# Attention and two quantized convolutions: values times exponentials by Strassen's seven products in column halves of TensorE

## The chip, the cores and the metric

The kernel runs on one core of one Trainium2 chip. The metric is the device time of one execution in microseconds (us), as the median of several runs.

Engines are called by their names in the profile: PE is TensorE's matmul, PEld its weight load, DVE VectorE, ACT ScalarE.

## The reference

The input is x, 16 images of 128 channels and 32 x 32 places (1024 columns when flat), all in fp32. The first layer is attention with 4 heads of 128 channels; the second is two quantized convolutions with batch norms over the whole batch.

```python
# layer 0, for each image and head: n, m are the 1024 places
q, k, v = split(einsum('bchw,oc->bohw', x, w_qkv) + b_qkv)
scores  = einsum('bnc,bcm->bnm', q, k) * c ** (-0.5)
attn    = softmax(scores, axis=-1)
out     = einsum('bnm,bmc->bnc', attn, v)
x       = einsum('bchw,oc->bohw', out_of_all_heads, w_out) + b_out + x
# layer 1
out = conv3x3(act_quant(x), weight_quant(w1))       # 4 bits, so exact in bf16
out = batchnorm(out, gamma1, beta1)                 # statistics over all 16 images
out = conv3x3(act_quant(out), weight_quant(w2))
x   = batchnorm(out, gamma2, beta2) + x
```

## The kernel before

It is already tuned. The weights of queries and keys are folded into one matrix (`at_sb`), those of values and output projection into another (`bt_sb`). Each of the 64 heads then needs: u from x (2 products of 128 x 128 weights by 512 columns), scores of 8 key blocks (16 products), exponentials on ScalarE, and values times exponentials (16 products); the values of all heads of an image cost 8 more. All of these are fp32. VectorE adds the exponentials up for the softmax's denominator and normalises. The first convolution of an image runs in between, in bf16; the second, after all images, takes the last 95 us. A list of steps places every small part of the work between scores and attends. These are the parts that the change touches, with cuts:

```python
xp, vp   = pool("x", 3), pool("vo", NCH + 3)        # NCH = 8 key blocks
ep, esp  = pool("e", 4), pool("es", 2)
ps_s = pool("ps_s", 2, space=PSUM)                  # tiles of N columns, two banks each
ps_a = pool("ps_a", 1, space=PSUM)                  # two accumulators of HALF
ps_m = pool("ps_m", 2, space=PSUM)

def project_v(b, j):
    ps = ps_m.tile([P, NH * P], F32, tag="mm", name=f"psv_{b}_{j}")
    nc.tensor.matmul(ps, lhsT=xt[b][:, ts(j, P)], rhs=bt_sb..., start=True, stop=True)
    vos[b, j] = vp.tile([P, NH * P], F32, tag="vo", name=f"vo_{b}_{j}")
    nc.vector.tensor_copy(vos[b, j], ps)

def scores(g, j):
    ps = ps_s.tile([P, N], F32, tag="s", name=f"pss_{g}_{j}")
    for m, (key, queries) in enumerate(parts):       # two halves of the queries
        last = nc.tensor.matmul(ps[:, ts(m, HALF)], lhsT=xt[b][:, ts(key, P)],
                                rhs=us[g][:, queries], start=True, stop=True)
    e = ep.tile([P, N], F32, tag="e", name=f"e_{g}_{j}")
    exps[:] = [nc.scalar.activation(e, ps, AF.Exp).ins]
    # ...

def attend(g, j):
    for m in range(NHF):
        nc.tensor.matmul(psa[g][m], lhsT=vos[b, j][:, ts(h, P)], rhs=e[:, ts(m, HALF)],
                         start=(j == 0), stop=(j == NCH - 1))
    # ... VectorE: es[g] += e

def six_products(p, s, i):        # first convolution, two images p at a time, F(4,3) by columns
    m = four_products(...)        # 4 bf16 products of 256 columns
    # ... seven or more VectorE operations that put the outputs together
```

Of the kernel before, what the change touches and what calls it, by code (L numbers as in the profile page):

```python
# [17 lines left out]
FIRST = 24.0  # L18
# [9 lines left out]

SUM_LIMIT = 1e20

# [160 lines left out]
def fast_path(  # L191
    nc, tc, x, wqk, wvo, bo, bnp, x1d, out, bo_sb, bnp_sb, quad, wq, sc, flag, conv_weights,
    constants,
):

# [38 lines left out]
    y2 = [keep.tile([P, 2, N], F32, name=f"y{b}") for b in range(0, B, 2)]  # L234
    ys = [y2[b // 2][:, b % 2] for b in range(B)]
# [109 lines left out]
    def check_sums():  # L345

        sums_range(B - 1)
        ok = keep.tile([P, 2], F32, name="ok")
        low, high = keep.tile([P, 1], F32, name="low"), keep.tile([P, 1], F32, name="high")
        nc.vector.tensor_reduce(low, ext[:, 0, :], AX.X, ALU.min)  # L350
        nc.vector.tensor_reduce(high, ext[:, 1, :], AX.X, ALU.max)
        nc.vector.tensor_scalar(ok[:, 0:1], low, 1.0 / SUM_LIMIT, None, ALU.is_ge)
        nc.vector.tensor_scalar(ok[:, 1:2], high, SUM_LIMIT, None, ALU.is_le)
        bad = keep.tile([P, 1], F32, name="bad")
        nc.vector.tensor_tensor(bad, ok[:, 0:1], ok[:, 1:2], ALU.mult)
        nc.vector.tensor_scalar(bad, bad, -1.0, 1.0, ALU.mult, ALU.add)
        worst = keep.tile([P, 1], F32, name="worst")
        nc.gpsimd.partition_all_reduce(worst, bad, P, bass_isa.ReduceOp.max)
        nc.vector.tensor_copy(flag, worst[0:1, :])

    with ExitStack() as ph:
        pool = lambda name, bufs, **kw: ph.enter_context(tc.tile_pool(name=name, bufs=bufs, **kw))
        once = pool("once", 1)
        xp = pool("x", 3)
        up = pool("u", 2)
        vp = pool("vo", NCH + 3)
        ep = pool("e", 4)
        esp = pool("es", 2)
        avp = pool("av", 2)
        smp = pool("small", 4)  # L370
        rbp = pool("rb", 1)
        rest = pool("rest", 1)
        accp = pool("acc", 1)
        ps_s = pool("ps_s", 2, space=PSUM)
        ps_a = pool("ps_a", 1, space=PSUM)
        ps_m = pool("ps_m", 2, space=PSUM)

        xt, us, vos, es, avs, psa, accs = {}, {}, {}, {}, {}, {}, {}
        exps, sums_added, scored, attended, quantized = [], [], [], [], []
        heads = [(b, h) for b in range(B) for h in range(NH)]  # L380

# [24 lines left out]
        def warm_up(n):  # L406
# [3 lines left out]
            for _ in range(n):  # L410
                nc.tensor.matmul(ps, lhsT=ones[:, 0:P], rhs=ones, start=True, stop=True)
# [4 lines left out]
        bt_sb = once.tile([P, NH, P], F32, name="bt_sb")  # L416

        def fold_a(h):
            wq_h, wk_h, bq_h = wqk_sb[:, h, 0:P], wqk_sb[:, h, P : 2 * P], wqk_sb[:, h, 2 * P :]
            ps = ps_m.tile([P, P + 1], F32, tag="mm", name=f"ps_a_{h}")  # L420
            bias = ps[:, P:]
            if h == 0:

                bias = ps_a.tile([P, 1], F32, tag="a1", name="ps_a_bias")
            nc.tensor.matmul(ps[:, 0:P], lhsT=wq_h, rhs=wk_h, start=True, stop=True)
            nc.tensor.matmul(bias, lhsT=wk_h, rhs=bq_h, start=True, stop=True)
# [3 lines left out]
        def fold_b():  # L430
            ps = ps_m.tile([P, NH, P], F32, tag="mm", name="ps_b")
            for h in range(NH):
                nc.tensor.matmul(
                    ps[:, h, :],
                    lhsT=wvo_sb[:, h, 0:P],
                    rhs=wvo_sb[:, h, P : 2 * P],
                    start=True,
                    stop=True,
                )
            nc.scalar.copy(bt_sb, ps)  # L440

        def fold_bo():
            ps = ps_m.tile([P, 1], F32, tag="mm", name="ps_bo")
            for h in range(NH):
                nc.tensor.matmul(
                    ps,
                    lhsT=wvo_sb[:, h, P : 2 * P],
                    rhs=wvo_sb[:, h, 2 * P :],
# [5 lines left out]
        bo2_sb = once.tile([P, 1], F32, name="bo2_sb")  # L454

        def project_u(g, hf):
            b, h = heads[g]
            if hf == 0:
                us[g] = up.tile([P, N], F32, tag="u", name=f"u_{g}")
            ps = ps_m.tile([P, HALF], F32, tag="mm", name=f"psu_{g}_{hf}")  # L460
            nc.tensor.matmul(  # L461
                ps, lhsT=at_sb[:, h, :], rhs=xt[b][:, ts(hf, HALF)], start=True, stop=True
            )
            dst = us[g][:, ts(hf, HALF)]
            if hf == 0:
# [6 lines left out]
        def project_v(b, j):  # L472
            ps = ps_m.tile([P, NH * P], F32, tag="mm", name=f"psv_{b}_{j}")
            nc.tensor.matmul(  # L474
                ps,
                lhsT=xt[b][:, ts(j, P)],
                rhs=bt_sb.rearrange("p h o -> p (h o)"),
                start=True,
                stop=True,
            )  # L480
            vos[b, j] = vp.tile([P, NH * P], F32, tag="vo", name=f"vo_{b}_{j}")
            nc.vector.tensor_copy(vos[b, j], ps)  # L482

        def scores(g, j):

            b, h = heads[g]
            ps = ps_s.tile([P, N], F32, tag="s", name=f"pss_{g}_{j}")
            if g == LAST:
                i, keys = group_step(j)
                lo, hi = GROUPS[i]  # L490
                parts = [(key, slice(lo, hi)) for key in keys]
            else:
                parts = [(j, ts(m, HALF)) for m in range(NHF)]
            for m, (key, queries) in enumerate(parts):
                last = nc.tensor.matmul(  # L495
                    ps[:, ts(m, N // len(parts))],
                    lhsT=xt[b][:, ts(key, P)],
                    rhs=us[g][:, queries],
                    start=True,
                    stop=True,  # L500
                )
            scored[:] = [last.ins]
            e = ep.tile([P, N], F32, tag="e", name=f"e_{g}_{j}")
            if (g, j) == (LAST, NCH - 1):
                for m in range(NHF):
                    nc.scalar.activation(e[:, ts(m, HALF)], ps[:, ts(m, HALF)], AF.Exp)
            else:
                exps[:] = [nc.scalar.activation(e, ps, AF.Exp).ins]  # L508
            es[g, j] = e

        def attend(g, j):
            b, h = heads[g]
            e = es[g, j]
            if j == 0:
                psa[g] = [
                    ps_a.tile([P, HALF], F32, tag=f"a{m}", name=f"psa_{g}_{m}") for m in range(NHF)
                ]
            for m in range(NHF):
                nc.tensor.matmul(  # L519
                    psa[g][m],  # L520
                    lhsT=vos[b, j][:, ts(h, P)],
                    rhs=e[:, ts(m, HALF)],
                    start=(j == 0),
                    stop=(j == NCH - 1),
                )
            if j == 1:
                es[g] = esp.tile([P, N], F32, tag="es", name=f"es_{g}")
                nc.vector.tensor_tensor(es[g], es.pop((g, 0)), es.pop((g, 1)), ALU.add)  # L528
            elif j > 1:
                added = nc.vector.tensor_tensor(es[g], es[g], es.pop((g, j)), ALU.add)  # L530
                sums_added[:] = [added.ins]
            if j == NCH - 1:
                avs[g] = avp.tile([P, N], F32, tag="av", name=f"av_{g}")
                nc.vector.tensor_copy(avs[g][:, ts(0, HALF)], psa[g][0])
                nc.scalar.copy(avs[g][:, ts(1, HALF)], psa[g][1])  # L535
                es[g, "part"] = quadrant_sums(es.pop(g))
# [13 lines left out]

        def inverse_sums(g, part, cut):
# [3 lines left out]
            if g == LAST:  # L555
# [3 lines left out]
                for i in range(w):  # L559
                    product = nc.tensor.matmul(  # L560
                        ps, lhsT=quad, rhs=part[:, ts(i, n)], start=(i == 0), stop=(i == w - 1)
                    )
                attended[:] = [product.ins]
                nc.vector.reciprocal(rinv, ps)
            else:
# [5 lines left out]
                nc.vector.tensor_reduce(total, side.rearrange("p a k -> p k a"), AX.X, ALU.add)  # L571
                nc.vector.reciprocal(rinv[0:Q, :], total)
# [8 lines left out]
        def normalise(g):  # L581
            b, h = heads[g]
            rb = inverse_sums(g, es.pop((g, "part")), slice(0, N))
# [6 lines left out]
            nc.vector.tensor_tensor(accs[b], accs[b], av, ALU.add)  # L590
            if h == NH - 1:
                nc.vector.scalar_tensor_tensor(xt[b], accs.pop(b), bo2_sb, xt[b], ALU.add, ALU.add)
                nc.sync.dma_start(out=x1d[b], in_=xt[b])
            elif g == LAST - 1:
                nc.vector.scalar_tensor_tensor(x1, accs.pop(b), bo2_sb, xt[b], ALU.add, ALU.add)
# [3 lines left out]
        LAST = len(heads) - 1  # L599
        GROUPS = [(0, HALF), (HALF, 3 * N // 4), (3 * N // 4, N)]  # L600
        FIRST_STEP = [0, NCH // 2, 3 * NCH // 4, NCH]
        x1 = rest.tile([P, N], F32, name="x1")
        sides, rbs = [], {}

        def group_step(j):

            i = max(k for k in range(len(GROUPS)) if FIRST_STEP[k] <= j)
            wide = N // (GROUPS[i][1] - GROUPS[i][0])
            return i, [wide * (j - FIRST_STEP[i]) + m for m in range(wide)]

        def attend_group(j):
            b, h = heads[LAST]
            e = es.pop((LAST, j))
            i, keys = group_step(j)
            n = GROUPS[i][1] - GROUPS[i][0]
            if j == FIRST_STEP[i]:
                ps = ps_a.tile([P, HALF], F32, tag=f"a{i % NHF}", name=f"psa_{LAST}_{i}")
                psa[LAST, i] = ps[:, 0:n]
                if i % NHF == 0:
# [724 lines left out]
```

## Time and profile before

| | before |
|---|---|
| time, median of 2 runs | 2105.22 us (2104.58 to 2105.87) |
| TensorE busy | 98% of the span |
| VectorE busy | 1508 us, 72% |
| ScalarE busy | 726 us, 35% |
| interval from one image's residual to the next | 124.85 us |
| second convolution, first product to the end | 94.6 us |

The busy table, the slices and the main groups of instructions are in the prediction below and are read there. Four more groups matter for the change. In the view of groups by shape, a line gives: source line, engine, operation, output<-input, shapes, number of instructions | busy us, mean ns of one | idle us of the engine just before them, and what ended it.

```profile
L482 DVE COPY vo<-psv 128x512 f32<-128x512 f32 x128 | 88.1, 689 | 194.7 <-PE psv L474 194.7
...
L753 DVE TENSOR_TENSOR tiles<-work 128x256 bf16<-128x256 bf16 x168 | 38.8, 288 | 0.0
L785 DVE TENSOR_TENSOR six<-wino 128x512 f32<-128x512 f32 x42 | 28.8, 686 | 0.0
L762 PE MATMUL psw<-tiles,wino 128*128 128x256 bf16 x184 | 27.6, 273 | 0.0
```

The first is the copy of the values to SBUF, on VectorE. The next two are the largest pieces of the first convolution's transforms on VectorE; all of its pieces together, over the seven pairs of images, are some 265 us, 18.9 us an image. The last is that convolution's products: only 27.6 us of TensorE. So the old first convolution was very cheap on TensorE and dear on VectorE.

### The profile page before, as it was taken

To read this page: it belongs to the slowest core of one execution; us is meant where nothing else is said; L and a number is where in the kernel's file an instruction comes from. 1 tells how busy PE (TensorE), PEld (TensorE's weight loads), DVE (VectorE), ACT (ScalarE), POOL (GpSimd) and SP (SyncE) were. 2 spreads that over 40 slices of the span, in tenths; PEclk is the share of its full clock that TensorE was granted. 3 is DMA by queue.
4 is the path that set the end of the run, shared out by engine and by line. 5 is a ranking of instruction groups with operands and counts; after the bars stand their busy time and mean duration, and the time that the engine had idled before them with its cause. 6 is when DMAs were issued, how large, how long until landed. Compare 5 with 4: busy or idle time off the path is not lost. (4 is left out here: it accounts for less than half of the span.)

```text
span 2103.3 us, 14858 instructions
## 1 busy us (share of the span) xinstructions
PE 2070.2 (98%) x5184; PEld 933.2 (44%) x5185; DVE 1508.2 (72%) x2434; ACT 726.4 (35%) x832; POOL 21.3 (1%) x29
## 2 busy tenths in 40 slices
PE   9999999999999999999999999999999999999994
PEld 4444444444444444444444444444444444444451
DVE  4775577766687676876769657776668767687888
ACT  2333233333333323333333323333333332333375
POOL 0000000000000000000000000000000000000020
PEclk9999999999999999999999999999999999999997
DMA  2000000000000000000000000000000000000044
GB/s 62 12 20 0 0 20 1 20 0 10 10 0 20 0 20 0 0 21 0 20 0 21 0 0 20 1 20 0 8 12 0 20 1 10 0 0 10 0 170 162
DMA packets 11155, 36.83 MB, mean 18 GB/s; under 512 B 1344, under 2 KB 1728, under 8 KB 11072
## 3 DMA queue, kind: packets, MB, share of 16 engines
q1 hardware_dynamic: 7872, 25.76, 3.2%
q10 hardware_dynamic: 3200, 10.03, 1.6%
q8 instruction: 43, 0.70, 0.1%
q14 instruction: 40, 0.33, 0.1%
HBM read 19.01 MB, written 16.78 MB: 17 GB/s over the span
## 5 line engine op out<-in xcount | busy, mean ns | idle before, releaser
L508 ACT ACTIVATE e<-pss 128x1024 f32<-128x1024 f32 x511 | 522.8, 1023 | 1287.6 <-PE pss L495 1267.6
L495 PE MATMUL pss<-u,x 128*128 128x512 f32 (+1 forms) x2064 | 962.4, 589 | 0.0
L519 PE MATMUL psa<-e,vo 128*128 128x512 f32 x2016 | 947.8, 592 | 0.0
L530 DVE TENSOR_TENSOR es<-es,e 128x1024 f32<-128x1024 f32 x378 | 461.6, 1221 | 293.8 <-ACT e L508 292.5
L495 PEld LDWEIGHTS pss<-u,x 128*128 128x128 f32 x2064 | 392.1, 190 | 487.2 <-issue 471.2
L519 PEld LDWEIGHTS psa<-e,vo 128*128 128x128 f32 x2016 | 379.1, 190 | 458.7 <-issue 454.2
L482 DVE COPY vo<-psv 128x512 f32<-128x512 f32 x128 | 88.1, 689 | 194.7 <-PE psv L474 194.7
L461 PE MATMUL psu<-x,at_sb 128*128 128x512 f32 x256 | 131.1, 594 | 0.8 <-DMA x<-in_x_dram 0.7
L474 PE MATMUL psv<-bt_sb,x 128*128 128x512 f32 x256 | 130.2, 592 | 0.0
L466 DVE TENSOR_SCALAR u<-psu,au_sb 128x512 f32<-128x512 f32 x64 | 48.0, 750 | 51.2 <-PE psu L461 51.2
L542 DVE TRANSPOSE_TENSOR_REDUCE part<-es 128x32 f32<-128x1024 f32 (+1 forms) x66 | 80.6, 1221 | 2.2
L528 DVE TENSOR_TENSOR es<-e,e 128x1024 f32<-128x1024 f32 x63 | 76.9, 1220 | 6.4 <-ACT e L508 6.4
L578 DVE STREAM_TRANSPOSE rb<-sums 128x1024 f32<-128x1024 f32 (+1 forms) x66 | 79.9, 1211 | 1.5
L461 PEld LDWEIGHTS psu<-x,at_sb 128*128 128x128 f32 x256 | 48.6, 191 | 62.0 <-issue 58.6
L474 PEld LDWEIGHTS psv<-bt_sb,x 128*128 128x128 f32 x256 | 48.6, 190 | 61.2 <-issue 55.7
L589 DVE TENSOR_TENSOR av<-av,rb 128x1024 f32<-128x1024 f32 x47 | 57.5, 1223 | 1.9
L590 DVE TENSOR_TENSOR acc<-acc,av 128x1024 f32<-128x1024 f32 x47 | 57.3, 1219 | 0.5
L769 ACT ACTIVATE wino<-psw 128x512 f32<-128x512 f32 x92 | 49.8, 599 | 0.0
L535 ACT COPY av<-psa 128x512 f32<-128x512 f32 x63 | 36.9, 585 | 33.3 <-PE psa L519 33.3
L569 DVE COPY side<-part 32x32 f32<-32x32 f32 x252 | 42.9, 170 | 4.7
L276 PE MATMUL psc<-pad,wq 128*128 128x512 bf16 (+3 forms) x225 | 45.0, 357 | 0.3 <-DVE pad L1002 0.3
L468 ACT ACTIVATE u<-psu,au_sb 128x512 f32<-128x512 f32 x64 | 43.6, 682 | 2.4 <-PE psu L461 2.4
(172 smaller groups left out, 857.8 us busy)
## 6 DMA issues: line engine op xcount, KB each, us to landing
x_dram<-x SPq DMA_DIRECT2D x16, 512.0 KB, 2.6
x<-in_x_dram ACTq DMA_DIRECT2D x15, 512.0 KB, 3.7
res<-x_dram SPq DMA_DIRECT2D x1, 7680.0 KB, 23.7
out_dram<-y SPq DMA_DIRECT2D x11, 512.0 KB, 4.4
out_dram<-y SPq DMA_DIRECT2D x9, 256.0 KB, 2.3
raw<-in_cw_dram ACTq DMA_DIRECT2D x2, 576.0 KB, 3.7
res<-x_dram SPq DMA_DIRECT2D x1, 512.0 KB, 3.4
wqk_sb<-in_wqk_dram ACTq DMA_DIRECT2D x1, 385.5 KB, 3.1
```

The costliest lines, as they stand in the source:

```text
L461: nc.tensor.matmul(ps, lhsT=at_sb[:, h, :], rhs=xt[b][:, ts(hf, HALF)], start=True, stop=True)
L474: nc.tensor.matmul(ps, lhsT=xt[b][:, ts(j, P)], rhs=bt_sb.rearrange("p h o -> p (h o)"), start=True, stop=True,)
L482: nc.vector.tensor_copy(vos[b, j], ps)
L495: last = nc.tensor.matmul(ps[:, ts(m, N // len(parts))], lhsT=xt[b][:, ts(key, P)], rhs=us[g][:, queries], start=True, stop=True,)
L508: exps[:] = [nc.scalar.activation(e, ps, AF.Exp).ins]
L519: nc.tensor.matmul(psa[g][m], lhsT=vos[b, j][:, ts(h, P)], rhs=e[:, ts(m, HALF)], start=(j == 0), stop=(j == NCH - 1),)
L528: nc.vector.tensor_tensor(es[g], es.pop((g, 0)), es.pop((g, 1)), ALU.add)
L530: added = nc.vector.tensor_tensor(es[g], es[g], es.pop((g, j)), ALU.add)
L542: nc.vector.tensor_reduce(part, total.rearrange("p (k c) -> p k c", c=Q), AX.X, ALU.add, apply_transpose=True,)
L578: nc.vector.transpose(rb, rinv.unsqueeze(2).to_broadcast([P, n, Q]))
L589: nc.vector.tensor_tensor(av, av, rb, ALU.mult)
L590: nc.vector.tensor_tensor(accs[b], accs[b], av, ALU.add)
```

## The change

The intent is to take products off TensorE. Values times exponentials for two key blocks is a product of 2 x 2 blocks (two channel halves by two key blocks, times two key blocks by two query halves): eight half products. Strassen's algorithm, in Winograd's form, needs seven, for some sums of blocks before and after. A "half" here has 64 output channels and uses 64 of TensorE's 128 columns, so two halves have to run side by side for any of this to pay. Hence:

- Every fp32 product, scores and u and values as well, is issued as two products of 64 columns, one to each column half ("lane") of TensorE, and a chain of dependences (`product`) fixes the order of issue.
- The seven of a step alternate between the lanes, and the next step's begin with the other lane.
- VectorE forms the sums of exponentials T1 to T4 and of values S1, S2, S4 (S3 is folded into the weights); ScalarE copies half results across partitions, and VectorE adds up the outputs once a head. The last head stays without Strassen.
- To free VectorE, the first convolution becomes Winograd by row pairs alone: per image 12 products of 512 columns, and few transforms. The copies of values and u go to ScalarE.
- A step now needs seven blocks of exponentials, so buffers shrink: e from 4 to 2 (of another size), x 3 to 2, es 2 to 1, the small PSUM pool 2 banks to 1; scores get 3 banks of 512 columns, and accumulators 4.
- The first convolution's outputs of six images (9 to 14) go to DRAM and are loaded again for the second convolution.
- The test that guards the fast path also asks that the sums of an image don't differ by more than a factor of 8.

The diff, cut to its core:

```diff
-        xp = pool("x", 3)
+        xp = pool("x", 2)
-        vp = pool("vo", NCH + 3)
-        ep = pool("e", 4)
-        esp = pool("es", 2)
+        vp = pool("vo", 5)
+        ep = pool("e", 2)
+        esp = pool("es", 1)
+        evp = pool("ev", 1)
-        ps_s = pool("ps_s", 2, space=PSUM)
+        ps_s = pool("ps_s", 3, space=PSUM)
-        ps_m = pool("ps_m", 2, space=PSUM)
+        ps_m = pool("ps_m", 1, space=PSUM)
+        def product(out_, lhsT, rhs, start=True, stop=True):
+            with tc.issue_after(pe[0]) if pe else nullcontext():
+                done = nc.tensor.matmul(out_, lhsT=lhsT, rhs=rhs, start=start, stop=stop)
+            pe[:] = [done.ins]
+            return done
+        lane = [0]
+        def halves(out_, lhsT, rhs, start=True, stop=True):
+            for t in (lane[0], 1 - lane[0]):
+                done = product(out_[LANES[t]], lhsT(t), rhs, start, stop)
+            return done
 # ... scores of one step: two key blocks (c) by two query halves (m)
+            for i, (c, m) in enumerate(((0, 1), (1, 1), (0, 0), (1, 0))):
+                ps = ps_s.tile([P, HALF], F32, tag="s", name=f"pss_{g}_{k}_{i}")
+                score(ps, b, g, k + NK * c, ts(m, HALF))
+                exps[:] = [nc.scalar.activation(e[:, 2 * c + 1 - m], ps, AF.Exp).ins]
+            nc.vector.tensor_tensor(e[:, T3], e[:, B12], e[:, B22], ALU.add)
+            nc.vector.tensor_tensor(
+                e[:, T1 : T2 + 1 : T2 - T1], e[:, B12 : B11 + 1], e[:, B11 : T3 + 1 : T3 - B11], ALU.subtract
             )
+            nc.vector.tensor_tensor(e[:, T4], e[:, T2], e[:, B21], ALU.add)
 # ... attend: (accumulator, lane, value block, exponential block)
-            for m in range(NHF):
-                nc.tensor.matmul(
-                    psa[g][m],
-                    lhsT=vos[b, j][:, ts(h, P)],
-                    rhs=e[:, ts(m, HALF)],
+            seven = [(0, 0, A11, B11), (1, 1, A22, T4), (1, 0, A12, B21), (2, 1, S2, T2)]
+            seven += [(2, 0, S4, B22), (3, 1, S1, T1)]
+            if k % 2:
+                seven = [seven[i] for i in (1, 0, 3, 2, 5, 4)] + [(0, 1, S3, T3)]
             else:
+                seven += [(3, 0, S3, T3)]
+            for n, (bank, t, value, exponential) in enumerate(seven):
+                product(
+                    psa[g][bank][LANES[t]],
+                    v[:, value],
+                    e[:, exponential],
+                    start=(k == 0 or (n == 6 and k == 1)),
+                    stop=(k == NK - 1 or (n == 6 and k == NK - 2)),
                 )
+            lane[0] = 1 - lane[0]
 # ... first convolution, one image: 4 of these, 3 taps each
+        def rows_product(b, k):
+            ps = ps_m.tile([P, D, W], F32, tag="mm", name=f"psw_{b}_{k}")
+            for dx in range(3):
+                halves(
+                    ps,
+                    lambda t: weights1[k][:, dx, LANES[t]],
+                    works[b][:, k, :, dx : dx + W],
+                    start=(dx == 0),
+                    stop=(dx == 2),
+                )
 # ... images 9 to 14 by way of DRAM
+    AWAY = range(9, B - 1)
+        back = resp.tile([P, len(AWAY), N], F32, name="back")
+        nc.sync.dma_start(out=back, in_=y1d.rearrange("b c n -> c b n"))
```

## The prediction

> **What bounds the kernel now.** I read the page's busy table and slices first, then the costliest groups, then the timeline in the middle of the run, then the table by stretches. The page:
>
> ```profile
> PE 2070.2 (98%) x5184; PEld 933.2 (44%) x5185; DVE 1508.2 (72%) x2434; ACT 726.4 (35%) x832; POOL 21.3 (1%) x29
> PE   9999999999999999999999999999999999999994
> DVE  4775577766687676876769657776668767687888
> PEclk9999999999999999999999999999999999999997
> ```
>
> TensorE is busy in every slice but the last, at full granted clock. That alone does not prove a bound, since matmul spans overlap; the groups of instructions do more:
>
> ```profile
> L508 ACT ACTIVATE e<-pss 128x1024 f32<-128x1024 f32 x511 | 522.8, 1023 | 1287.6 <-PE pss L495 1267.6
> L495 PE MATMUL pss<-u,x 128*128 128x512 f32 (+1 forms) x2064 | 962.4, 589 | 0.0
> L519 PE MATMUL psa<-e,vo 128*128 128x512 f32 x2016 | 947.8, 592 | 0.0
> L530 DVE TENSOR_TENSOR es<-es,e 128x1024 f32<-128x1024 f32 x378 | 461.6, 1221 | 293.8 <-ACT e L508 292.5
> ```
>
> ScalarE waits 1268 us for TensorE's scores, VectorE 293 us for ScalarE, and the two large matmul groups wait for nothing. One fp32 product leaves two records (2016 records of psa are 63 heads x 8 key blocks x 2 halves x 2). The timeline gives the spacing:
>
> ```profile
> 1003.46 1.88 PE L495 MATMUL pss<-u,x 128*128 128x512 f32 x4
> 1005.17 1.02 PE L474 MATMUL psv<-bt_sb,x 128*128 128x512 f32 x2
> 1006.03 1.88 PE L519 MATMUL psa<-e,vo 128*128 128x512 f32 x4
> 1007.75 1.88 PE L495 MATMUL pss<-u,x 128*128 128x512 f32 x4
> ```
>
> Four records take 1.717 us from start to start, so a record takes d = 0.429 us of the array and a full fp32 product 0.858 us, not the 1.18 us that two records of 592 ns seem to say. The table by stretches shows where this regime ends:
>
> ```profile
> 1000.00:1500.00 500.00, 500.00 (x1202) 222.82 (x1201) 357.63 (x568) 165.55 (x188) 0.00 (x0) 1.00 0.03 9
> 2050.00:2104.00 54.00, 22.89 (x113) 10.55 (x111) 45.12 (x74) 29.76 (x37) 2.42 (x2) 0.75 0.41 157
> ```
>
> Columns are length, busy us (count) of PE, PEld, DVE, ACT, POOL, clock, DMA share, GB/s. Attention is 100% TensorE up to about 2008 us; the second convolution after it, 95 us, hangs largely on VectorE. The output-projected residual of an image (line 592) recurs from 149.0 to 1896.9 us in 14 intervals: 124.85 us an image. Products alone explain it: 64 scores + 64 attends + 8 u + 8 v = 144 x 0.858 = 123.6 us, and 24 convolution products of 256 bf16 columns x 0.11 us, half of a pair's 24, add 1.3. So there is no slack on TensorE: a product taken away is time taken away.
>
> **What the Trainium skill says.** "FP8 and Floating Point Precision", TensorE Precision Notes: true fp32 takes 4 passes. The trace agrees: bf16 products of 512 columns in the second convolution (18 in 4.13 us with the pipeline's tail) cost near 0.22 us, a quarter of 0.858. "TensorEngine Tiling (Array Packing)", Key Properties: column tiles operate independently, loads and matmuls of different tiles in parallel, but changing the mode drains the engine. "TensorE: Matmul & The Clock Gate", Part 3: matmuls start and end in program order, and three column tiles of 32 gave 2.38x. The trace before has no column tile, so it neither confirms nor denies these two; the whole change rests on them. "VectorE: DVE Perf Modes", in its section on the TRN2 errata, gives (N+151)/0.96 ns for fp32 tensor_tensor adds; 1224 ns for 1024 elements, and the trace has 1221.
>
> **The change part by part.**
>
> *Values times exponentials.* For 63 of 64 heads, key blocks are paired; each of 4 steps a head forms seven products of 64 output columns where eight half products (four full ones) stood. If two column halves really run together, a step costs 3.5 x 0.858 instead of 4 x 0.858. 252 steps x 0.5 x 0.858 = **-108.2 us**.
>
> *All other fp32 products become pairs of halves.* Same work if the halves run together. An fp32 product is two records in sequence, and starts are in order; so the first record of one lane overlaps the second record of the other, a stagger of one record. This keeps both lanes full if, and only if, lanes strictly alternate. In the built order they do: steps with even k run lanes 0,1,0,1,0,1,0, the next half products start with lane 1, odd k runs 1,0,1,0,1,0,1. So 0 us, on the assumption above.
>
> *First convolution.* 24 products of 256 columns per image pair (1.3 us an image) become 12 of 512 columns per image: 12 x 0.216 = 2.6 us. 15 images: 15 x 12 x 0.216 = 38.9, less 184 products x 0.11 = 20.2: **+19 us**. The bf16 pairs are single records, so the stagger is lost on entering a block of six halves and rebuilt on leaving it: about 0.2 us of one lane and 0.43 of the other idle, 0.3 us a block, 60 blocks: **+19 us**, an estimate that I trust by half.
>
> *ScalarE.* 1008 exponentials at 594 ns (the page's 512-column form) = 599; evacuations 252 x 0.585 = 147; 315 half-partition copies, reckoned also at 0.585, = 184; values 128 x 0.6 = 77; u 127 x 0.68 = 87; the convolution's 60 x 0.6 = 36. With some 90 for the rest, 1220 us, 60%. Not a bound on average. At the change of heads four evacuations come before the exponentials of the next step; three score banks give TensorE 2.6 us, and I work out the first exponential done at about 2.4 us after the last attend. Just enough.
>
> *VectorE.* Per step the new T sums take 0.686 + 1.221 + 0.686 = 2.59 us; per head 10.4, three sums of sums 3.7 (was 8.5), inverse sums 4.5 as before, recombination 4 x 0.686 = 2.7, normalise 2.1: 23.4 us, 93.8 an image. Values' S sums 4 x (0.42 + 0.69) = 4.4, residual and quantize 2.7, row transforms 1.7, output 2.6, statistics and extremes 1.9: 107 us an image in spans. TensorE will need 136 x 0.858 + 2.6 + 1.3 = 120.6 us an image. Back-to-back spans on VectorE overlap by some 0.08 us (1.22 us ops start 1.14 to 1.17 apart), so its real load is near 97, 81%. It gives up 24 small transform operations an image pair and the value and u copies. **Added on the path: little, but bursts.** The head after an image's end has about 31 us of VectorE spans against 31 us of TensorE work. An attend comes 6 us after its exponentials, and its chain takes 2.6, so 3.5 us of backlog are covered. I allow 0.5 us an image, **+8 us**.
>
> *Six images in DRAM.* 3 MB out during attention where DMA is at 2%, and back before the residual's 7.7 MB, which landed in 24 us before. The ninth image is first needed about 20 us into the second convolution; 3 MB at the page's 170 GB/s takes 18 us. Hidden, barely: 0 us. Ratio test of sums: seven tiny operations, 0.
>
> Sum: 2105.2 - 108.2 + 19 + 19 + 8 = 2043 with the stagger losses whole, 2033 with half of them. I take **2036 us**.
>
> **Rivals.** (1) *Column halves do not overlap in fp32.* Then halves cost like wholes and the time nears 3900 us; a partial overlap of 85% would already cost 300. For: no trace here shows it. Against: the strict lane order is pointless unless this works. (2) *VectorE becomes the bound.* For: 107 against 120 us in spans, 100% in the head after an image. Against: overlapping spans, and the backlog allowance. If its chain were late by 2 us a head, +126 us, and the gain is gone: 2140. I hold 1 us a head (2085) possible. (3) *ScalarE and the single ps_m bank stall TensorE* at head changes: 0.5 us a head is +32 us, 2068. For: buffers shrink from double to single in many pools (e 4 to 2, values, ps_m 2 to 1). Against: 60% load. (4) *No bubbles at all*, bf16 pairs slide in: 2016 us.
>
> **Range and chances.** 2016 is the floor from counts; 2036 the middle; waits of up to 0.7 us a head put the upper end at 2080. Faster by over 2% means under 2064: I give it 0.8, since every step but the overlap itself is counted, and some 28 us of further waits fit in. Within 2%: 0.11. Slower: 0.09, nearly all rival 1 and a heavy rival 2.
>
> **What would show each step right or wrong.** In the changed kernel's timeline an attend's seven halves should start 3.0 us ahead of what follows and a step's four scores 3.43 us; if a half record lies far more than 0.43 us after the one before it, rival 1 holds. The interval of the residual should fall from 124.85 to about 120.6 us. The page should show VectorE near 88% in spans (about 1800 us) and ScalarE near 60%. In the waits, attend halves waiting for VectorE's T sums would be rival 2, scores waiting for exponentials rival 3; each should be under 20 us. The second convolution should still take about 95 us; if image nine waits for its reload, step six fails. The prediction is wrong if TensorE's halves run at another rate than d a record, or if these waits exceed half a us a head.

## The result, and the profile after

| | before | after |
|---|---|---|
| time, median of 2 runs | 2105.22 us | 2023.99 us (2023.41 to 2024.57) |
| ratio after / before | | 0.9614, 95% interval 0.9573 to 0.9655: faster |
| interval from one image's residual to the next | 124.85 us (149.0 to 1896.9 in 14) | 119.38 us (158.3 to 1829.6 in 14) |
| attention, to the second convolution's first product | 2008.7 us | 1928.5 us |
| second convolution | 94.6 us | 94.2 us |
| VectorE busy | 1508 us | 1722 us |
| ScalarE busy | 726 us | 1199 us |

A ratio is the mean time of one kernel's fast runs over that of the other's fast runs of the same rounds, so it is not quite the ratio of the medians. A control run of five rounds later gave 2023.67 us (below), and its results were correct.

The page after, its busy table and three of its slices (each digit a fortieth of the span, in tenths):

```profile
PE 1987.6 (98%) x9497; PEld 730.3 (36%) x9497; DVE 1722.2 (85%) x2642; ACT 1198.5 (59%) x2007; POOL 19.7 (1%) x29
...
PE   9999999999999999999999999999999999999994
...
DVE  5889888888888888888888888888888888878888
...
PEclk9999999999999999999999999999999999999997
```

TensorE is as full as before, at the same clock, but its span ends 81 us sooner. VectorE has gone from a mixed 4 to 8 to an even 8. The page's costliest groups:

```profile
L403 PE MATMUL pss<-u,x 128*64 128x512 f32 (+1 forms) x4128 | 1031.9, 589 | 1.6 <-ACT u L509 1.6
L403 PE MATMUL psa<-e,vo 128*64 128x512 f32 (+1 forms) x3624 | 922.4, 588 | 0.0
L551 ACT ACTIVATE e<-pss 128x512 f32<-128x512 f32 x1008 | 595.4, 596 | 380.7 <-PE pss L403 331.9
...
L555 DVE TENSOR_TENSOR e<-e 128x1024 f32<-128x1024 f32 x252 | 307.7, 1221 | 29.8 <-ACT e L551 21.6
L554 DVE TENSOR_TENSOR e<-e 128x512 f32<-128x512 f32 x252 | 172.2, 683 | 105.5 <-ACT e L551 101.7
```

A product of 64 columns takes the same 589 ns record as one of 128 did. There are twice as many score records (4128 for 2064), yet the time fell, so two of them do run at once. The two VectorE lines are the new T sums, at the prediction's durations. In both matmul groups the idle time is next to nothing. The timeline of TensorE in the middle of the run shows the rate:

```profile
1020.72 3.17 PE L403 MATMUL psa<-e,vo 128*64 128x512 f32 x13
1023.30 1.03 PE L403 MATMUL psw<-rows,middle 128*64 128x512 bf16 x5
1023.96 0.59 PE L403 MATMUL pss<-u,x 128*64 128x512 f32 x1
1024.17 0.38 PE L403 MATMUL psw<-rows,middle 128*64 128x512 bf16 x1
1024.38 3.60 PE L403 MATMUL pss<-u,x 128*64 128x512 f32 x15
1027.39 1.03 PE L403 MATMUL psw<-rows,middle 128*64 128x512 bf16 x5
```

Two blocks of six bf16 halves start at 1023.30 and 1027.39 us, 4.09 apart. Between the starts lie one such block and four scores. Four scores, 16 records in two lanes, take 8 x 0.429 = 3.43 us, so the block took 0.66 us: 3 x 0.216 is 0.65. Nothing was lost on entering or leaving it. The reason is in the third and fourth lines: the first record of the scores started at 1023.96, **before** the last record of the block (1024.17), which the program has ahead of it. The lane that had finished its bf16 halves went on with its scores; the other lane finished its own first. So each half follows its own sequence. (The records don't name the half; the spacing of their starts tells it.)

The table by stretches, for the first 100 us and for one image interval (length, then busy us and count of PE, PEld, DVE, ACT, POOL, then clock, DMA share, GB/s), of the kernel after:

```profile
0.00:100.00 100.00, 95.31 (x426) 43.19 (x428) 70.03 (x127) 47.66 (x81) 5.22 (x16) 1.00 0.12 33
985.20:1104.60 119.40, 119.40 (x572) 42.06 (x570) 102.52 (x153) 71.24 (x123) 0.00 (x0) 1.00 0.03 10
```

And of the kernel before, the first 100 us:

```profile
0.00:100.00 100.00, 98.09 (x250) 46.36 (x251) 62.21 (x114) 27.97 (x30) 6.54 (x16) 1.00 0.13 39
```

The interval of 119.38 us is nothing but work: 136 products x 0.858 + 12 x 0.216 = 119.3. In the steady state there isn't a wait of TensorE. The start is another matter: TensorE idles more in the first 100 us than it did. Counting the starts against the cost of each product, TensorE falls behind by 12.6 us there, where it fell behind by 5.1 us before: some 7.4 us of loss that no part of the prediction had (an estimate; counted again with the small products by their columns it is 7.7). The timeline of that stretch shows some of it:

```profile
43.32 1.12 PE L403 MATMUL psv<-bt_sb,x 128*64 128x512 f32 x4
44.38 0.61 PE L403 MATMUL ps_a<-wqk_sb 128*128 128x128 f32 x4
44.91 1.08 PE L403 MATMUL psu<-x,at_sb 128*64 128x512 f32 x4
46.78 3.65 PE L403 MATMUL pss<-u,x 128*64 128x512 f32 x16 [0.79 <-ACT u L509]
50.37 1.05 PE L403 MATMUL ps_bo<-wvo_sb 128*128 128x1 f32 x8
```

The brackets hold idle time and what ended it: the scores wait 0.79 us for u, which ScalarE copies just ahead of need. The `128*128` lines are the small weight products, left as full ones amid halves: eight records with a single column each (`ps_bo`) hold TensorE from 50.37 to 51.35 us.

Do the steady state's engines wait for one another at all? In the waits of the kernel after (engine, line, what it waited for: us in total, times, longest):

```profile
ACT e L551 <- DVE es L562: 46.9, 46, 2.7
...
PEld pss L403 <- ACT e L551: 17.8, 67, 0.7
```

In 46 heads ScalarE's first exponential of the third step waits for VectorE's sum over the first two steps (L562), 1 us at a time: there are two buffers of e, and this sum still reads the one that the third step needs. It reaches as far as the weight loads of scores (17.8 us in all), but the interval shows that it doesn't reach the matmuls. It is a warning, though, and two experiments below follow it up.

The whole difference adds up: 252 steps x 0.5 x 0.858 = -108.2; first convolution +18.7 (180 x 0.216 less 184 x 0.11); start +7.4, sum -82.1. Measured is -81.2; the 0.9 us between them are not assigned.

### The profile page after: what moved, and what is told of

Read it like the earlier page. It is cut to its first block, busy times and chain, and to the rows that moved or that the text cites. A ratio compares the mean times of both kernels' runs of the same rounds, so it can differ in the third digit from the quotient of the medians.

```text
span 2022.7 us, 24701 instructions
## 1 busy us (share of the span) xinstructions
PE 1987.6 (98%) x9497; PEld 730.3 (36%) x9497; DVE 1722.2 (85%) x2642; ACT 1198.5 (59%) x2007; POOL 19.7 (1%) x29
## 5 line engine op out<-in xcount | busy, mean ns | idle before, releaser
L403 PE MATMUL pss<-u,x 128*64 128x512 f32 (+1 forms) x4128 | 1031.9, 589 | 1.6 <-ACT u L509 1.6
L403 PE MATMUL psa<-e,vo 128*64 128x512 f32 (+1 forms) x3624 | 922.4, 588 | 0.0
L551 ACT ACTIVATE e<-pss 128x512 f32<-128x512 f32 x1008 | 595.4, 596 | 380.7 <-PE pss L403 331.9
L403 PEld LDWEIGHTS pss<-u,x 128*64 128x64 f32 x4128 | 351.6, 137 | 549.3 <-issue 493.4
L403 PEld LDWEIGHTS psa<-e,vo 128*64 128x64 f32 x3624 | 304.8, 137 | 483.5 <-issue 449.6
L555 DVE TENSOR_TENSOR e<-e 128x1024 f32<-128x1024 f32 x252 | 307.7, 1221 | 29.8 <-ACT e L551 21.6
L554 DVE TENSOR_TENSOR e<-e 128x512 f32<-128x512 f32 x252 | 172.2, 683 | 105.5 <-ACT e L551 101.7
L558 DVE TENSOR_TENSOR e<-e 128x512 f32<-128x512 f32 x252 | 174.0, 690 | 21.5 <-DVE e L555 0.5
L403 PE MATMUL psu<-x,at_sb 128*64 128x512 f32 x512 | 184.9, 599 | 1.0 <-DMA x<-in_x_dram 1.0
L403 PE MATMUL psv<-bt_sb,x 128*64 128x512 f32 x512 | 184.9, 592 | 1.0 <-ACT bt_sb L480 1.0
L564 DVE TENSOR_TENSOR es<-es,e 128x1024 f32<-128x1024 f32 x126 | 154.0, 1222 | 2.7
L562 DVE TENSOR_TENSOR es<-e,e 128x1024 f32<-128x1024 f32 x63 | 76.8, 1219 | 0.0
## 6 DMA issues: line engine op xcount, KB each, us to landing
back<-y_dram SPq DMA_DIRECT2D x1, 3072.0 KB, 11.4
```

What stands on the lines that cost most here:

```text
L403: done = nc.tensor.matmul(out_, lhsT=lhsT, rhs=rhs, start=start, stop=stop)
L551: exps[:] = [nc.scalar.activation(e[:, 2 * c + 1 - m], ps, AF.Exp).ins]
L554: nc.vector.tensor_tensor(e[:, T3], e[:, B12], e[:, B22], ALU.add)
L555: nc.vector.tensor_tensor(e[:, T1 : T2 + 1 : T2 - T1], e[:, B12 : B11 + 1], e[:, B11 : T3 + 1 : T3 - B11], ALU.subtract)
L558: nc.vector.tensor_tensor(e[:, T4], e[:, T2], e[:, B21], ALU.add)
L562: nc.vector.tensor_tensor(sides[g], es[g, 0][:, T4 : T3 + 1], mine, ALU.add)
```

## The experiments

Theory A was the prediction's: records start in program order, so both halves stay full only while the program strictly alternates between them, and what enters or leaves a bf16 block leaves a bubble. Its rival B, from the trace after: each half follows its own sequence and the order matters only within some reach. All twelve runs were, but for e3, correct.

### e1_no_flip: one pair of neighbours in the same half at each step

```diff
-            lane[0] = 1 - lane[0]
```

> The lane order is no longer strictly alternating: each of the 252 steps has one place where two neighbouring half products use the same column half; nothing else changes. Theory A (starts are in order across the halves, as the prediction said: the other half idles one record d = 0.429 us at each such place): 252 x 0.429 = +108 us, about 2132 us, the whole gain gone. Rival B (each half runs its own queue and takes its next product as soon as it is free; the trace after shows bf16 records of one half starting between records of the other half with no idle time): +0 us, 2024 to 2030 us. In between, for example +54, would mean a short look-ahead.

Measured: 2024.83 us (2023.56 to 2027.61), ratio to before 0.9619 (0.9603 to 0.9635), against 2023.99 for the change itself. The rule of strict alternation is refuted: the line that keeps it does nothing for the time.

### e2_sorted: four of one half, then three of the other

```diff
-            lane[0] = 1 - lane[0]
             # the seventh product added as before, then:
+            seven.sort(key=lambda p: p[1])
             # start and stop flags bound to S3 in place of n == 6
```

> Each attend issues all its products of one half first, then all of the other (4 and 3, or 3 and 4), so five same-half neighbours a step. Theory A (in order across halves): 252 x 5 x 0.429 = +541 us, about 2565 us. Rival B (independent halves with enough look-ahead): near 2024 us, at most some tens more. If run 1 was free and this one is not, the look-ahead is one or a few products deep.

Measured: 2194.41 us (2193.78 to 2197.94), ratio 1.043 (1.0412 to 1.0447). Order does matter, by 170 us or 0.68 us a step, but far less than if the halves took strict turns. The timeline of TensorE of this run:

```profile
1003.24 1.23 PE L403 MATMUL psu<-x,at_sb 128*64 128x512 f32 x4
1004.10 3.65 PE L403 MATMUL psa<-e,vo 128*64 128x512 f32 x12
1007.53 0.59 PE L403 MATMUL pss<-u,x 128*64 128x512 f32 x1
```

Twelve records of attends take 3.43 us from 1004.10 to 1007.53; two to a slot of 0.429 they would take 2.57. In the single records, the first four stand alone, 0.429 us apart up to 1005.8 us, and the rest come in pairs. The other half's first product stands behind four of the first half in the program, and it started only when two of the four were through. Waits for the T sums, which this order asks for at other times, hardly explain it: the attends' weight loads waited 7.6 and 7.5 us in all for the two later sums, never over 0.3.

### e9_pairs and e10_triples: how far ahead does the other half find its work?

```diff
             # e9, in place of the alternation; no flip
+            order = (0, 2, 1, 3, 4, 5, 6) if k % 2 else (0, 2, 1, 3, 4, 6, 5)
             # e10
+            order = (6, 0, 2, 4, 1, 3, 5) if k % 2 else (0, 2, 4, 1, 3, 5, 6)
+            seven = [seven[i] for i in order]
             # start and stop flags bound to S3 in place of n == 6
```

> How far does a column half look ahead? Each attend issues at most two neighbouring products of the same half (0,0,1,1,0,0,1). In run e2, where four or three of one half stood together, the trace shows four records (two products) of one half alone before the other half's next one started. Theory (look-ahead of about four records, two products): pairs are free, 2024 to 2028 us. Rival (a look-ahead of one product only, as run 1 would also allow): 252 x 0.2 to 0.4 = +50 to +110 us.

> As the run of pairs, with three neighbouring products of one half. Theory (look-ahead of two products): the third stands in the way for up to one product each time; e2 with four cost 0.68 us a step, so 0.1 to 0.4 us a step here, 2050 to 2120 us. Rival (cost comes from something else in e2, such as the later T sums being asked for in another order): 2024 us or 2190 us.

Measured: pairs 2047.63 us (2045.74 to 2049.30), triples 2043.40 us (2043.02 to 2046.04): +23.6 and +19.4 us over the change, 0.09 and 0.08 us a step. Both expectations missed. Pairs were not free, and triples were not dearer than pairs. Runs of two and three in one half cost a little, runs of four a lot. Why the little: in these runs the starts of the two halves' fp32 records are shifted against each other, mostly by 0.06 to 0.16 us (medians 0.10 for pairs and 0.06 for triples, from 100 to 1800 us), where 96% of the change's lie within 0.01 us. A small shift alone is free: e1 has one of 0.04 us in some of its records. What the cost of pairs and triples comes from stays open.

### e3_eight: the eighth half product put back (wrong results on purpose)

```diff
-            lane[0] = 1 - lane[0]
-            if k % 2:
-                seven = [seven[i] for i in (1, 0, 3, 2, 5, 4)] + [(0, 1, S3, T3)]
-            else:
-                seven += [(3, 0, S3, T3)]
+            seven += [(3, 0, S3, T3), (0, 1, S3, T3)]
             # start and stop flags without the special case of n == 6
```

> An eighth half product a step (the S3 T3 product goes to both accumulators; the result is wrong on purpose), halves strictly alternating. It takes away Strassen's saving and leaves everything else, the sums on VectorE included. If the halves run fully together and TensorE has no slack, 252 x 0.429 = +108 us, 2132 us, that is 27 us above the kernel before (first convolution +19, start +7). If part of the time was another engine's, less than +108.

Measured: 2131.73 us (2129.48 to 2132.66), ratio 1.0123 (1.0106 to 1.0140): +107.7 us over the change, where the prediction's main term is 108.2. The result is wrong, since S3 T3 is counted in two places. This measures the term by itself: half a product a step is worth what it costs at full rate. It shows too that the rest of the change, without the seventh-for-eighth, would be 1.2% slower than the kernel before (the interval lies wholly above 1).

### e4_full_uv: u and values by full products amid halves

```diff
-            halves(ps, lambda t: at_sb[:, h, LANES[t]], xt[b][:, ts(hf, HALF)])
+            product(ps, at_sb[:, h, :], xt[b][:, ts(hf, HALF)])
-            halves(ps, lambda t: xt[b][:, ts((k + NK * c) * 2 + t, PH)], weights)
+            product(ps, xt[b][:, ts(k + NK * c, P)], weights)
```

> Only u and the values are projected by full 128-column products again, 252 of them, in the midst of half products. If a change between full and half columns costs nothing: 2024 us. If the array drains at each change, as the Trainium skill's tiling page says: the three full products of the first 70 us each came 0.31 us late in the trace after, so 250 x 0.31 to 0.5 us = +80 to +130 us, 2100 to 2155 us.

Measured: 2176.24 us (2175.48 to 2178.94), ratio 1.0336 (1.0319 to 1.0354): +152.2 us. There are 256 such products (512 records of u and 512 of values, four to a pair of halves), so a full product among halves costs 0.60 us more, dearer than expected. The timeline of TensorE of this run:

```profile
1001.68 3.60 PE L403 MATMUL pss<-u,x 128*64 128x512 f32 x14
1005.21 1.13 PE L403 MATMUL psu<-x,at_sb 128*128 128x512 f32 x2
1006.26 1.94 PE L403 MATMUL psa<-e,vo 128*64 128x512 f32 x8
```

In the single records two losses can be told apart. The last four score records before u start at 1003.83, 1003.87, 1004.26 and 1004.69 us: the last two have no partner. Seven and eight half products stand between one full product and the next, 15 in all, and the odd one has a half of the array idle beside it for 0.858 us, worth 0.43 of the whole. Then u's two records start at 1005.21 and 1005.74, the first halves after it at 1006.27 and the second at 1006.75: gaps of 0.52, 0.53, 0.52 and 0.47 for 0.429, together 0.34 us. The period from this u to the one before it (997.14) is 8.07 us, against 7.29 of counted work, and 0.34 + 0.43 is 0.77 of that 0.78. The rest of the trace bears this out: at 219 full products between 100 and 1850 us the four gaps come to 0.34 us over their 4 x 0.429 in the mean, and before 62% of them the last half stands alone. 0.34 + 0.62 x 0.43 is 0.61, and 0.60 was measured.

With this the change would have lost outright, though the number of products is the same. It is why every product of the stage, even where Strassen isn't used, is cut into halves: a half product left over can then pair with whatever comes next.

### e5_dve_one_more and e6_dve_two_more: how much room has VectorE?

```diff
             nc.vector.tensor_tensor(e[:, T3], e[:, B12], e[:, B22], ALU.add)
+            nc.vector.tensor_tensor(e[:, T3], e[:, B12], e[:, B22], ALU.add)    # e6: twice more
```

> VectorE computes T3 twice in each of the 252 steps (the second changes nothing): 16 x 0.61 = +9.7 us of VectorE an image, on 102.5 busy us of the 119.4 us an image takes after the change. Theory A (only the mean load counts, bursts are covered by the lag between exponentials and attend): 112 of 119.4, the time stays at 2024 to 2028 us. Rival B (bursts after an image's end already use up the lag): waits of TensorE appear, 1 to 3 us an image, 2040 to 2070 us.

> T3 three times: +19.4 us of VectorE an image, 121.9 against 119.4 us. VectorE becomes the bound under every theory. If its time is the sum of its busy time: 15.75 x 2.5 = +39 us, about 2063 us; more if idle gaps that wait for ScalarE cannot be filled (some 7 us of idle an image now): up to 2024 + 15.75 x 10 = 2180 us.

Measured: 2080.49 us (2079.47 to 2083.25; ratio 0.988) and 2227.91 us (2222.56 to 2235.64; ratio 1.059): +56.5 and +204 us. Both went beyond even the dearer expectation. In e5, 11 us an image more of VectorE's spans (16 x 0.69; 9.0 us of busy time, by 1864.3 us in the page for 1722.2) gives 3.6 us an image more in time (56.5 / 15.75 images), although VectorE isn't full. The table by stretches of e5 and then of e6, for the stretch shown before:

```profile
985.20:1104.60 119.40, 117.34 (x554) 52.98 (x552) 108.21 (x165) 68.67 (x118) 0.00 (x0) 1.00 0.03 10
...
985.20:1104.60 119.40, 112.32 (x512) 51.61 (x514) 107.88 (x162) 62.57 (x107) 0.00 (x0) 0.97 0.03 10
```

VectorE is busy 108 of 119 us, TensorE no longer always. In e6 VectorE is no busier, and the granted clock is lower, 0.97 here. So e6's 204 us are not VectorE's alone: the clock's mean fell by 0.020 (0.973 for 0.993), which over 2222.5 us is 44 us of TensorE's time, an estimate. The argument below rests on e5, whose clock was 0.993. Its waits:

```profile
ACT e L551 <- DVE es L563: 80.6, 45, 2.1
PEld pss L403 <- ACT e L551: 79.9, 82, 2.9
PE pss L403 <- ACT e L551: 33.8, 32, 2.0
```

The chain is: VectorE's sums hold a buffer of e, the exponentials wait for it, the score banks aren't freed, TensorE waits. The last line is the time in which no matmul ran; what makes up the rest of the 56 us these lines don't tell. It is not the attends' wait for the T sums that the prediction's second rival named: that comes to 1.2 us in all.

### e12_one_more_3e: e5's extra sum, with a third buffer of e

```diff
+            nc.vector.tensor_tensor(e[:, T3], e[:, B12], e[:, B22], ALU.add)
-        ep = pool("e", 2)
+        ep = pool("e", 3)
-    AWAY = range(9, B - 1)
+    AWAY = range(5, B - 1)      # ten images in DRAM, to make room
```

> The run with one more VectorE operation a step (2080 us), now with three buffers for the exponentials in place of two; to make room ten images wait in DRAM in place of six, which can cost a few us at the start of the second convolution. In that run TensorE waits for score banks, those for the exponentials, and those for VectorE's sums of sums, which hold the exponentials' buffer. If that chain is the cause, the third buffer takes most of the +56 us away: 2026 to 2045 us. If the late T sums or VectorE's total load are the cause: still about 2080 us.

Measured: 2032.77 us (2030.01 to 2035.32), ratio 0.9658 (0.9643 to 0.9673). The third buffer takes back 48 of e5's 56 us. Of the remaining 9, 3.5 lie in the second convolution (97.6 us in this run's trace, 94.1 in the control's), with the longer reload; attention ends at 1930.6 us, in the control at 1930.7 (but this trace is of e12's fastest run, 2030.01 us, and the control's of its slowest, 2026.64). The other 5.5 us are not assigned. One line of its waits:

```profile
PEld pss L403 <- ACT e L551: 35.1, 113, 1.0
```

The weight loads' wait is down from 79.9 to 35.1 us and no single one is over 1.0. So most of e5's loss came with the number of buffers: with three, the same VectorE work costs 9 us. (The ten images in DRAM were not run alone.)

### e7_conv_twice: the first convolution's products doubled

```diff
-            for dx in range(3):
+            for dx in (0, 1, 2, 0, 1, 2):
```

> Every product of the first convolution by row pairs is made twice (the second pass starts anew, so the result is right): 15 x 12 more products of 512 bf16 columns in halves. With no slack on TensorE and no loss between blocks: 15 x 12 x 0.216 = +39 us, 2063 us. The prediction's rule of 0.3 us a block does not enter (the blocks are the same 60). Less would mean that this convolution fits in gaps.

Measured: 2063.39 us (2062.05 to 2065.67), ratio 0.980 (0.9785 to 0.9815): +39.7 us over the control of its batch (2023.67, below) for 180 more pairs of halves, 0.22 us each. (The second first tap starts the accumulator anew, so the result stays correct.) The size of this term was right, and longer bf16 blocks have no more bubble than short ones.

### c_after and e11_start: the control, and a version with less loss at the start

```diff
             # c_after: no edit
             # e11: the small weight products of heads 1 to 3, of the values and of the bias as halves
-                product(ps[:, h, :], wvo_sb[:, h, 0:P], wvo_sb[:, h, P : 2 * P])
+                halves(ps[:, h, :], lambda t: wvo_sb[:, h, LANES[t]], wvo_sb[:, h, P : 2 * P])
             # and, for the first step of the first two heads, scores of the query half that is ready first
+            if k == 0 and g < 2:
+                parts = ((0, 0), (1, 0), (0, 1), (1, 1))
             # and the first values one score later
```

> The changed kernel once more, unaltered, as the control of this batch: 2024 us, within 0.2%.

> An attempt to win back part of the slower start: in the first 100 us TensorE loses 12.6 us against its counted work after the change, 5.2 before. Here the small products of weights after the first are half products too (no change of columns amid half products: each cost 0.31 us late), the first head and the second begin with the queries whose u is ready first (waits of 0.8 and 0.96 us), and the first values come one score later (1.04 us). If these waits lie on the path: 3 to 5 us less, 2019 to 2021 us. If they are taken up by later waits: 2024 us.

Measured in the same five rounds: control 2023.67 us (2022.24 to 2026.64; ratio 0.961), e11 2020.97 us (2018.17 to 2022.64; ratio 0.9597). The difference of the means is 3.4 us; paired by rounds it is 3.3 with an interval of about 3 on either side, so it is likely but small. The trace agrees: TensorE falls behind by 9.3 us in the first 100, in place of 12.6. This is the best version, faster than both kernels, over the change by some 0.15% if the difference holds.

## Why the prediction was right, point by point

- **Column halves overlap in fp32: right.** Seven halves, 14 records, take 3.00 us, four scores 3.43, as the prediction said they should, and e3 measures the main term at 107.7 us for the 108.2 predicted. Its first rival falls.
- **The first convolution's +19 us: right in size** (18.7 by count, and e7 measures 39.7 for what was counted as 38.9).
- **"starts are in order", lanes must "strictly alternate": wrong.** This is the step that failed. e1 breaks the alternation and costs nothing; in the trace after, a score's record starts ahead of a bf16 record that the program has earlier. Each half follows its own sequence; only four products of one half in a row cost much (e2).
- **Bubbles at bf16 blocks, +19 us trusted by half: wrong,** they are zero (0.66 us for 0.65). That is the fourth rival, "no bubbles at all", as far as this goes.
- **VectorE's bursts, +8 us: none measured,** as the interval has 0.05 us beyond its work. The load was well placed (1722 us of spans against "about 1800"), but the danger was elsewhere: e5 and e12 show it in the buffers of e, which the prediction had listed under its third rival, ScalarE and the small bank. In the change itself that rival shows as 17.8 us of waiting weight loads, under its limit of 20, and costs nothing. Another 11 us of VectorE work an image would have cost 56 us. Two sums of the second rival don't come out: from 2036, 126 us more are 2162 and not 2140, and 1 us a head is 2099 and not 2085.
- **Missing altogether: the start,** +7.4 us. The prediction worked from the steady state and took the first 100 us as unchanged. There u is copied just ahead of need, the values' folded weights pass through ScalarE, and the small weight products switch the array between whole and halves.
- **The drain on a change of mode** was quoted but given no cost. e4 gives one: 0.34 us for each full product amid halves, and 0.60 with the odd halves that it leaves without a partner.
- **Six images in DRAM: right, and not "barely".** The page's issues after, with KB and us from issue to landing, show

```profile
res<-x_dram SPq DMA_DIRECT2D x1, 7680.0 KB, 30.0
...
back<-y_dram SPq DMA_DIRECT2D x1, 3072.0 KB, 11.4
```

  The reload, issued at 1928.3 us, landed 11.4 us later; its first use is at 1951.2, 11.5 us after that. The estimate of 18 us came from the mean rate of a page slice and was too slow. The residual's load after it takes 30.0 us in place of 23.7, and the second convolution still takes 94 us.

So the predicted 2036 us was 12 us too high: 9.5 of bubbles and 8 of bursts that didn't come, less 7.4 at the start that did, leaves 10; the prediction's sum of 2033.5 was then taken as 2036, and 0.9 us is not assigned. That it came so near is in part luck: 17.5 us of waits that didn't come stood against 7.4 us that it had missed. What the experiments don't show is whether Strassen could have stood beside the old first convolution: that needed 18.9 us of VectorE an image where the new one needs 4.3 (63.8 us of groups over 15 images). With 102.5 of 119.4 us busy now, 14.6 more would be about 117. With 11 more, two buffers of e lost 56 us (e5) and three lost 9 (e12), so with the buffers as built I believe not; but it was argued, not run.

## What to carry to other kernels

Where TensorE is full, take products away, but first count what the sums that replace them need of the other engines and of buffers: here the seven-for-eight seems to have needed the time that the first convolution gave back to VectorE (argued, not run), and with a little more work on VectorE one buffer too few cost 48 us while VectorE still had 11 of 119 us idle. When column halves are used, use them for everything in the stage, since each full product amid halves cost 0.60 us here, nearly half of it for want of a partner, and keep runs in the same half short; strict alternation isn't needed. Look at the start of the kernel apart from its steady state: it was the one loss that the counts of the steady state could not show.

## What the Trainium skill lacked or had wrong

- "TensorE: Matmul & The Clock Gate", Part 3, has matmuls monotone in program order for start and end. Here a score's record of one column half started at 1023.96 us, ahead of a bf16 record of the other half at 1024.17 that is earlier in the program. As far as the spacing of the records tells, the order holds within a half, not between halves.
- The same page gives no reach for this. The runs: no cost for two neighbours in one half once a step (2024.83 us), 0.08 to 0.09 us a step for runs of two or three, 0.68 us a step for a run of four and one of three.
- "TensorEngine Tiling (Array Packing)", Key Properties, says that a change of tiling mode drains the engine, without a figure. Here a full fp32 product amid halves stretched the four gaps around it by 0.34 us together, and cost 0.60 us more in the mean (152.2 us / 256), as it also leaves odd halves without a partner.
- No page says that fp32 products run in two column halves at full rate. Here 14 half records took 3.00 us, 7 slots of 0.429, each slot what a full record takes alone.
- "TensorE: Matmul & The Clock Gate", LDWEIGHTS (loading the stationary operand), has P / 1.2 ns for P columns, so 107 ns for 128 and 53 for 64. The records' spans here were 190 ns (128 columns) and 137 ns (64 columns) in fp32, and 97 and 110 ns in bf16: 64 columns cost far more than half of 128. They lay beside the matmuls and cost nothing here.
